# A selective-scan block on one core: the scan writes into PSUM, and its product is taken there

## The chip, the core and the metric

The kernel runs on one core of a Trainium2 chip. The core has a matrix engine (TensorE, PE in the profile), a vector engine (VectorE, DVE), an activation engine (ScalarE, ACT) and a general engine (GpSimd, POOL); DMAs are mostly issued from a fifth queue (SP). Each engine works through its own queue in order. The metric is the device time of one execution in microseconds (us).

## The reference

The input is 4096 rows of 1024 numbers. The block is a half feed-forward step, a Mamba step and the same feed-forward step again, each with a layer norm and a residual:

```python
x = x + 0.5 * ffn(layernorm(x))
x = x + mamba(layernorm(x))
x = x + 0.5 * ffn(layernorm(x))
```

The feed-forward step multiplies by a weight matrix rounded to -1, 0 or 1 times a scale, and adds a bias. The Mamba step is what the change touches:

```python
u, z = split(x @ W_in.T)                  # 1024 channels each
u = silu(conv_b + causal convolution of u over 4 rows)
dt_r, B, C = split(u @ W_xproj.T)         # 64, 16 and 16 columns
dt = softplus(dt_r @ W_dt.T + b_dt)
# for each of 16 states n and each channel d, along the rows t:
h[t] = exp(dt[t] * A[d, n]) * h[t-1] + dt[t] * B[t, n] * u[t]
y[t] = sum over n of h[t] * C[t, n]
out = ((y + u * Dskip) * silu(z)) @ W_out.T
```

So for each state there is a linear recurrence along the rows (the exponential is its decay), and a product of the whole history h with C.

## The kernel before

The rows are cut into 16 chunks of 256 rows (T). Channels lie on the 128 partitions, in 8 blocks; a chunk is worked in two halves of 4 blocks (HB). The history of a state is a tile `h` of 4 x 256 columns in SBUF. For each chunk, half and state:

- `fetch` loads the state's rows of B and C, spread over all partitions (`bc`, 6 buffers), through SP.
- `enter` (L934, L941) lets GpSimd write u * dt * B into `h` and add to each block's first column what comes over from the chunk before.
- `decaying` (L913) lets ScalarE write the decays, exp(dt * A), into a PSUM tile `da` of 2 blocks (512 columns, one of 3 such buffers). Two `da` tiles, j = 0 and 1, serve one state. Column 0 of each block is left out: it stays 0, set once before the loop (L847), so that a scan over two blocks starts anew at each of them.
- `recur` (L966) lets VectorE scan 512 columns: h = da * h_before + h, in place in `h`. After that the `da` buffer is free.
- `leave` (L949) lets ScalarE copy the last column of all 4 blocks of `h` into `state`, which the next chunk's `prepare` reads.
- `left` (L981) lets VectorE take the product of the whole `h` (1024 columns) with C into a tile `p`. It stands one state behind: the product of state n - 1 comes between the two scans of state n.
- `paired` (L996) adds, for states 0, 4 and 8, the product before to this one, on VectorE. It too stands one state behind, after the second scan.
- `summed` (L1019) lets TensorE transpose the remaining products and sum them in PSUM; `gate` (L1036) multiplies by silu(z) on VectorE.

All the rest runs beside it: the feed-forward steps (`ffn`: L456 and L458 split the normalized rows into two parts, L499 multiplies, L479 adds the result), the norm statistics (L393 to L412), the convolution (L550 and L560), the products with W_in (L616 and L675) and W_out (L758, added at L729), the delta step (L720), `prepare` (L860 to L873) and `skipping` (L899, u * Dskip as a further product).

The order of all instructions on each engine is fixed when the program is built. `Streams` is a small planner: each piece of work is a generator that asks for an engine for a planned time (`dve(1132)` asks VectorE for 1132 ns) and not before a given time. The planner always gives the engine to the request that can start first; among equals, to the one of lowest rank. The ranks (DECAY, ENTER, RECUR and so on), REACH (planned time from one engine to another), the LATE constants (added to due times), HOLD (how long an engine may be kept free for a request of lower rank) and the planned DMA times (5000 and 6000 ns) set that order; at run time only semaphores hold an engine. A second rule keeps instructions marked "port" on VectorE and GpSimd apart in the plan. There are 3 PSUM buffers `bank` for everything that TensorE writes apart from the sums.

Of the kernel before, what the change touches and what calls it, by code (L numbers as in the profile page):

```python
# [32 lines left out]
F32 = mybir.dt.float32  # L33
F32R = mybir.dt.float32r
AF = mybir.ActivationFunctionType
ALU = mybir.AluOpType
# [16 lines left out]
FULL, PASS, TURN = 0.844, 0.455, 0.855  # L53
REACH = 160
ISSUE, ADDED = 950, 6000
SWITCH = 1300

LATE_P, LATE_X, LATE_D, LATE_N = 300, 300, 1200, 300
PAIRED = (0, 4, 8)

DECAY, ENTER, SUM, PREPARE, RECUR, GATE = 4, 3, 1, 0, 5, 0
FFN_A, NORM, U_PART, CONV, DELTA, OUT, FFN_C = 1, 1, 3, 2, 2, 2, 3

HOLD = 250, 0, 0, 500
Z = 2, 4


class Streams:
# [32 lines left out]
    def run(self):  # L101
        hold = dict(zip(("PE", "DVE", "ACT", "POOL"), HOLD))
        while self.streams:
            todo = sorted(((self.start(s[2]), s[1], i) for i, s in enumerate(self.streams)))
            for at, rank, i in todo:
# [72 lines left out]
def macaron_mamba_kernel(  # L178
# [165 lines left out]
    def streamed(load, n, ahead, rank):  # L344

        queue = []

        def fill():
            for i in range(n):
                yield lambda: 0 if len(queue) < ahead else INF  # L350
                w = yield from weights.take()
                load(i, w)
                queue.append((order.now + 5000, w))

        order.spawn(fill(), rank)
        return queue
# [53 lines left out]
    def normed(c, ln, xn, t, at):  # L410
        end = yield act(D + 210, at)
        nc.scalar.activation(  # L412
            xn[t],
            x_tiles[c, t],
            AF.Identity,
            scale=ln[:, 28 + t : 29 + t],
            bias=ln[:, 32 + t : 33 + t],
        )
        return xn[t], end + REACH + LATE_N

# [21 lines left out]
    def ffn(c, which, rank, at, tiles=range(TT)):  # L442
# [3 lines left out]
        def split(t):  # L446
# [6 lines left out]
            def cut(g, pt, at_):  # L453
                part_hi, part_lo = (flat(p_[:, 4 * g : 4 * g + 4, :]) for p_ in (hi, lo))
                end = yield act(512, at_)
                nc.scalar.copy(part_hi, pt)  # L456
                end = yield dve(640, end + REACH)
                nc.vector.tensor_tensor(part_lo, pt, part_hi, ALU.subtract)  # L458
                banks.put(pt, end)
                ends.append(end)  # L460
                if len(ends) == NB // 4:
                    ready["parts", key, t] = end + REACH + LATE_N
                    parts[t] = lo, hi
# [195 lines left out]
    def gates(c, xT):  # L659
        queue = streamed(z_weights, NB, 2, Z[0])  # L660
        for half in range(2):
# [110 lines left out]
    def back():  # L772
        for c in range(NC - 1):
            yield OUT
            yT = []
            for half in range(2):
                if half:
                    yield from when("product", c, 1, 0)
                    queue = streamed(lambda i, w: out_weights(i // 2, i % 2, w), NB, 3, OUT)
                yT.append((yield from us.take()))  # L780
                yield from turned(c, half, yT[half])
# [62 lines left out]


    for _, da in decays.free:
        nc.vector.memset(da[:, :, 0], 0.0)  # L847
    halves = [(c, half) for c in range(NC) for half in range(2)]
# [54 lines left out]
    def decaying():  # L903
        for c, half, n in items:
# [3 lines left out]
            for j in range(2):  # L908
                da = yield from decays.take()
                for i in range(2):  # L910
                    b = 2 * j + i
# [13 lines left out]
    def enter():  # L925
        for c, half, n in items:
# [15 lines left out]
            entering[c, half, n] = h  # L942
            ready["enter", c, half, n] = end + REACH
            if n + 1 == NST:
                overs.put(over[c, half], end)

    def leave(c, half, n, h, at):
        end = yield act(100, at)
        nc.scalar.copy(state[:, half, :, n], h[:, :, T - 1])  # L949
        ready["left", c, half, n] = end  # L950
        if n + 1 == NST:
            ready["state", c, half] = end

    def recur():
        behind = None
        for c, half, n in items:
# [4 lines left out]
            for j in range(2):  # L961
# [3 lines left out]
                rows_ = flat(h[:, 2 * j : 2 * j + 2, :])  # L965
                nc.vector.tensor_tensor_scan(rows_, flat(da), rows_, 0.0, ALU.mult, ALU.add)  # L966
                decays.put(da, end)
                if behind and j == 0:
                    yield from left(*behind)
                elif behind:  # L970
                    yield from paired(*behind[:3])
            order.spawn(leave(c, half, n, h, end + REACH), ENTER)
            behind = c, half, n, h
        yield from left(*behind)
        yield from paired(*behind[:3])

    def left(c, half, n, h):
        bc = coming.pop((c, half, n))
        p = yield from products.take()
        end = yield dve(1132, 0, True)  # L980
        nc.vector.tensor_tensor(p, h, bc[:, 1:2, :].to_broadcast([P, HB, T]), ALU.mult)  # L981
# [138 lines left out]
```

## Time and profile before

| what | value |
|---|---|
| time, median of 2 runs | 2623.18 us (2622.4 and 2623.95) |
| time of the profiled execution | 2623.95 us |
| its span, first to last instruction | 2622.2 us |
| mean granted TensorE clock | 0.980 |
| decay exponentials on ScalarE, L913 | 2048, 474 ns each |
| scans on VectorE, L966 | 1024, 1206 ns each |
| products on VectorE, L981 | 512, 1355 ns each |
| pair sums on VectorE, L996 | 96, 2014 ns each |
| entering products on GpSimd, L934 | 512, 2391 ns each |
| state copies on ScalarE, L949 | 512, 188 ns each |

The profile comes from one execution. A group line names the line of the kernel, the engine, the operation, what it writes and reads, the shapes and the count; after the bar stand the busy time in us and the mean duration of one in ns, and after the second bar the idle time of the engine just before such instructions, with what ended it. The first scan starts at 102.1 us and the last at 2576.3 us; between them the 16 chunks follow each other with a period of about 156 us.

### The profile page before, as it was taken

To read this page: it belongs to the slowest core of one execution; us is meant where nothing else is said; L and a number is where in the kernel's file an instruction comes from. 1 tells how busy PE (TensorE), PEld (TensorE's weight loads), DVE (VectorE), ACT (ScalarE), POOL (GpSimd) and SP (SyncE) were. 2 spreads that over 40 slices of the span, in tenths; PEclk is the share of its full clock that TensorE was granted. 3 is DMA by queue.
4 is the path that set the end of the run, shared out by engine and by line. 5 is a ranking of instruction groups with operands and counts; after the bars stand their busy time and mean duration, and the time that the engine had idled before them with its cause. 6 is when DMAs were issued, how large, how long until landed. Compare 5 with 4: busy or idle time off the path is not lost. (4 is left out here: it accounts for less than half of the span.)

```text
span 2622.2 us, 38817 instructions
## 1 busy us (share of the span) xinstructions
PE 2473.1 (94%) x13314; PEld 2118.7 (81%) x13314; DVE 2467.7 (94%) x2532; ACT 1953.2 (74%) x4084; POOL 1746.9 (67%) x1433
## 2 busy tenths in 40 slices
PE   5987999999999999999999999999999999999867
PEld 4776778888888888888888888888888888888756
DVE  5589999999999999999999999999999999999994
ACT  3678678787778878777797878779787887876652
POOL 0456767767676776767677676766767677776772
PEclk9999899999999999999999999999999999999988
DMA  5544445556544555555555544555654455554451
GB/s 166 156 134 129 149 128 174 158 176 181 165 150 141 177 165 176 160 169 151 156 164 181 173 152 153 160 166 163 188 165 146 141 175 159 177 175 151 122 156 37
DMA packets 218541, 410.68 MB, mean 157 GB/s; under 512 B 19172, under 2 KB 85860, under 8 KB 218344
## 3 DMA queue, kind: packets, MB, share of 16 engines
q1 hardware_dynamic: 209128, 374.65, 44.2%
q0 software_dynamic: 9216, 33.56, 6.9%
q8 instruction: 105, 1.72, 0.3%
q14 instruction: 92, 0.75, 0.1%
HBM read 390.82 MB, written 17.31 MB: 156 GB/s over the span
## 5 line engine op out<-in xcount | busy, mean ns | idle before, releaser
L934 POOL TENSOR_TENSOR h<-u,bc 128x1024 f32<-128x1024 f32 x512 | 1224.2, 2391 | 565.8 <-ACT da L913 257.7
L913 ACT ACTIVATE da<-dt,pr 128x255 f32<-128x255 f32 x2048 | 946.3, 474 | 432.1 <-DVE h L966 398.9
L966 DVE TENSOR_TENSOR_SCAN h<-da,h 128x512 f32<-128x512 f32 x1024 | 1215.5, 1206 | 31.8 <-ACT da L913 22.3
L981 DVE TENSOR_TENSOR p<-h,bc 128x1024 f32<-128x1024 f32 x512 | 694.0, 1355 | 0.1
L1019 PE MATMUL y<-ident,p 128*128 128x128 f32 x3584 | 480.7, 279 | 74.2 <-DVE p L981 59.9
L1019 PEld LDWEIGHTS y<-ident,p 128*128 128x128 f32 x3584 | 423.0, 144 | 136.8 <-DVE p L981 81.1
L616 PE MATMUL bank<-xT,weight 128*128 128x259 f32 x2048 | 477.4, 386 | 11.1 <-issue 7.6
L675 PE MATMUL bank<-weight,xT 128*128 128x256 f32 x2048 | 478.0, 382 | 2.9 <-DMA weight<-in_w_in 1.0
L758 PE MATMUL bank<-weight,u 128*128 128x256 f32 x2016 | 464.1, 380 | 2.9 <-DMA weight<-in_w_out 2.8
L616 PEld LDWEIGHTS bank<-xT,weight 128*128 128x128 f32 x2048 | 384.0, 192 | 73.5 <-issue 10.8
L675 PEld LDWEIGHTS bank<-weight,xT 128*128 128x128 f32 x2048 | 377.5, 191 | 51.8 <-DVE x L479 2.9
L758 PEld LDWEIGHTS bank<-weight,u 128*128 128x128 f32 x2016 | 373.9, 191 | 49.5 <-ACT da L913 2.5
L941 POOL TENSOR_TENSOR h<-h,over 128x4 f32<-128x4 f32 x512 | 343.0, 670 | 33.7
L499 PE MATMUL bank<-wf,lo 128*128 128x512 f32 x976 | 255.7, 404 | 3.8 <-DVE lo L458 3.7
L499 PE MATMUL bank<-wf,hi 128*128 128x512 f32 x976 | 244.7, 393 | 0.0
L499 PEld LDWEIGHTS bank<-wf,lo 128*128 128x128 f32 x976 | 181.1, 190 | 44.3 <-DVE lo L458 8.0
L560 DVE SCALAR_TENSOR_TENSOR u<-bank,pr,u 128x256 f32<-128x256 f32 x384 | 176.4, 467 | 38.7 <-ACT u L550 36.4
L499 PEld LDWEIGHTS bank<-wf,hi 128*128 128x128 f32 x976 | 181.5, 188 | 37.2 <-issue 0.3
L996 DVE TENSOR_TENSOR p<-p,p 128x1024 f32<-128x1024 f32 x96 | 193.4, 2014 | 0.0
L395 POOL TENSOR_SCALAR ln<-ln 128x1 f32<-128x1 f32 x96 | 35.8, 373 | 182.0 <-ACT tmp L393 178.7
L428 PE MATMUL bank<-ident,tmp 128*128 128x128 f32 x756 | 114.5, 285 | 33.1 <-ACT tmp L412 24.0
L428 PEld LDWEIGHTS bank<-ident,tmp 128*128 128x128 f32 x756 | 93.1, 146 | 52.8 <-ACT tmp L412 30.2
(98 smaller groups left out, 1966.5 us busy)
## 6 DMA issues: line engine op xcount, KB each, us to landing
bc<-bcd SPq DMA_DIRECT2D x512, 256.0 KB, 3.7
weight<-in_w_in SPq DMA_DIRECT2D x128, 512.0 KB, 4.6
weight<-in_w_in SPq DMA_DIRECT2D x256, 256.0 KB, 5.6
weight<-in_w_out SPq DMA_DIRECT2D x128, 512.0 KB, 4.1
x<-hbias POOLq DMA_DIRECT2D x64, 512.0 KB, 9.4
x<-in_x SPq DMA_DIRECT2D x32, 512.0 KB, 5.0
out<-x SPq DMA_DIRECT2D x30, 512.0 KB, 4.5
weight<-in_w_ffn SPq DMA_DIRECT2D x5, 512.0 KB, 7.2
```

The lines of the kernel that those rows point to most:

```text
L428: nc.tensor.matmul(pt[:, j * P : (j + 1) * P], xn[:, k * P : (k + 1) * P], ident, start=(j == 0), stop=(j == 3), is_transpose=True, skip_g ...
L499: nc.tensor.matmul(pf, x[:, k, :], wf[:, k, cols], start=(x is lo and k == 0), stop=(x is hi and k == NB - 1),)
L616: nc.tensor.matmul(pp[:, : KER - 1 + T], wt[:, k, :], xT[:, k, PAD - KER + 1 : PAD + T], start=(k == 0), stop=(k == NB - 1),)
L675: nc.tensor.matmul(pp[:, t, :], xT[:, k, PAD + t * P : PAD + (t + 1) * P], wt[:, :, i, :], start=(k == 0 and t == 0), stop=(k == NB - 1), ...
L758: nc.tensor.matmul(po[:, t, :], yT[:, b, t * P : (t + 1) * P], wt[:, b, :], start=(half == 0 and t == 0 and b == 0), stop=(half == 1 and b ...
L913: nc.scalar.activation(da[:, i, 1:], dt[c, half][:, b, 1:], AF.Exp, scale=a_neg[:, half * HB + b, n : n + 1],)
L934: nc.gpsimd.tensor_tensor(h, u[c, half], bc[:, 0:1, :].to_broadcast([P, HB, T]), ALU.mult)
L941: nc.gpsimd.tensor_tensor(h[:, :, 0], h[:, :, 0], over[c, half][:, :, n], ALU.add)
L966: nc.vector.tensor_tensor_scan(rows_, flat(da), rows_, 0.0, ALU.mult, ALU.add)
L981: nc.vector.tensor_tensor(p, h, bc[:, 1:2, :].to_broadcast([P, HB, T]), ALU.mult)
L996: nc.vector.tensor_tensor(flat(p), flat(p), flat(q), ALU.add)
L1019: nc.tensor.matmul(y[t][:, b * P : (b + 1) * P], p[:, b, t * P : (t + 1) * P], ident, start=(first and b == 0), stop=(n == NST - 1 and b = ...
```

## The change

The scan now writes its result over the decays in the PSUM tile `da` and no longer into `h`. The product with C reads it there, 512 columns at a time, directly behind each scan on VectorE; so there are 1024 products of 512 columns in place of 512 of 1024, and the pair sum follows the second product of its own state. `h` is free after the second scan. The state copy is made per `da` tile, 2 blocks at a time, by ScalarE (1024 copies in place of 512), and `da` is free after both the copy and the product. Since the scan overwrites column 0 of each block, ScalarE zeroes the two columns anew in each `da` tile before the exponentials, by a copy from a tile of zeros (1024 copies of 128 x 2). With it come other planning constants: REACH 300 in place of 160, ranks, LATE constants, later planned DMA times, a term TABLE that puts ScalarE requests for another function table 300 ns later in the planner's choice, three z weights ahead in place of two, and the output weights fetched from product 12 of the second half on in place of product 0. The diff, without the lines that only rename or move:

```diff
-REACH = 160
-ISSUE, ADDED = 950, 6000
+REACH = 300
+ISSUE, ADDED = 950, 9000
-LATE_P, LATE_X, LATE_D, LATE_N = 300, 300, 1200, 300
+LATE_P, LATE_X, LATE_D, LATE_E = 300, 700, 1200, 300
-DECAY, ENTER, SUM, PREPARE, RECUR, GATE = 4, 3, 1, 0, 5, 0
-FFN_A, NORM, U_PART, CONV, DELTA, OUT, FFN_C = 1, 1, 3, 2, 2, 2, 3
-
-HOLD = 250, 0, 0, 500
+DECAY, ENTER, SUM, PREPARE, RECUR, GATE = 1, 1, 1, 0, 5, 1
+FFN_A, NORM, U_PART, CONV, DELTA, OUT, FFN_C = 1, 0, 3, 2, 2, 2, 4
+
+TABLE = 300
+HOLD = 250, 0, 100, 500
...
-            todo = sorted(((self.start(s[2]), s[1], i) for i, s in enumerate(self.streams)))
+            todo = []
+            for i, s in enumerate(self.streams):
+                w = s[2]
+                other = not callable(w) and w[0] == "ACT" and w[3] not in (None, self.table)
+                todo.append((self.start(w) + other * TABLE, s[1], i))
+            todo.sort()
...
-                queue.append((order.now + 5000, w))
+                queue.append((order.now + 6500, w))
...
-        return xn[t], end + REACH + LATE_N
+        return xn[t], end + REACH
...
-                    ready["parts", key, t] = end + REACH + LATE_N
+                    ready["parts", key, t] = end + REACH
...
-        queue = streamed(z_weights, NB, 2, Z[0])
+        queue = streamed(z_weights, NB, 3, Z[0])
...
-                    yield from when("product", c, 1, 0)
+                    yield from when("product", c, 1, 12)
...
-    for _, da in decays.free:
-        nc.vector.memset(da[:, :, 0], 0.0)
+    none = const.tile([P, 2], F32, name="none")
+    nc.vector.memset(none, 0.0)
...
                 da = yield from decays.take()
+
+                yield act(0)
+                nc.scalar.copy(da[:, :, 0], none)
...
-            ready["enter", c, half, n] = end + REACH
+            ready["enter", c, half, n] = end + REACH + LATE_E
...
-    def leave(c, half, n, h, at):
-        end = yield act(100, at)
-        nc.scalar.copy(state[:, half, :, n], h[:, :, T - 1])
-        ready["left", c, half, n] = end
-        if n + 1 == NST:
+    def leave(c, half, n, j, da, at):
+
+        blocks = slice(2 * j, 2 * j + 2)
+        end = yield act(0, at)
+        nc.scalar.copy(state[:, half, blocks, n], da[:, :, T - 1])
+        if j and n + 1 == NST:
             ready["state", c, half] = end
+        decays.put(da, max(end, (yield from when("multiplied", c, half, n, j))))
...
                 da = decay.pop((c, half, n, j))
                 end = yield dve(1132)
                 rows_ = flat(h[:, 2 * j : 2 * j + 2, :])
-                nc.vector.tensor_tensor_scan(rows_, flat(da), rows_, 0.0, ALU.mult, ALU.add)
-                decays.put(da, end)
-                if behind and j == 0:
-                    yield from left(*behind)
-                elif behind:
-                    yield from paired(*behind[:3])
-            order.spawn(leave(c, half, n, h, end + REACH), ENTER)
-            behind = c, half, n, h
-        yield from left(*behind)
-        yield from paired(*behind[:3])
-
-    def left(c, half, n, h):
-        bc = coming.pop((c, half, n))
-        p = yield from products.take()
-        end = yield dve(1132, 0, True)
-        nc.vector.tensor_tensor(p, h, bc[:, 1:2, :].to_broadcast([P, HB, T]), ALU.mult)
-        bcs.put(bc, end)
-        product[c, half, n] = p
-        if n not in PAIRED:
-            ready["product", c, half, n] = end + REACH + LATE_P
-        order.spawn(give(c, half, n, h, end), ENTER)
+                nc.vector.tensor_tensor_scan(flat(da), flat(da), rows_, 0.0, ALU.mult, ALU.add)
+                order.spawn(leave(c, half, n, j, da, end + REACH), 0)
+                yield from left(c, half, n, j, da)
+            hs.put(h, end)
+
+    def left(c, half, n, j, da):
+        bc = coming[c, half, n]
+        if not j:
+            product[c, half, n] = yield from products.take()
+        p = product[c, half, n][:, 2 * j : 2 * j + 2, :]
+        end = yield dve(605)
+        nc.vector.tensor_tensor(p, da, bc[:, 1:2, :].to_broadcast([P, 2, T]), ALU.mult)
+        ready["multiplied", c, half, n, j] = end
+        if j:
+            bcs.put(coming.pop((c, half, n)), end)
+            if n not in PAIRED:
+                ready["product", c, half, n] = end + REACH + LATE_P
+            yield from paired(c, half, n)
...
-    def give(c, half, n, h, at):
-        end = yield from when("left", c, half, n)
-        hs.put(h, max(at, end))
```

More of the change, by code (lines that the diff above doesn't have):

```diff
@@ L942, in enter @@
             entering[c, half, n] = h
-            ready["enter", c, half, n] = end + REACH
+            ready["enter", c, half, n] = end + REACH + LATE_E
             if n + 1 == NST:
                 overs.put(over[c, half], end)
-    def leave(c, half, n, h, at):
-        end = yield act(100, at)
-        nc.scalar.copy(state[:, half, :, n], h[:, :, T - 1])
-        ready["left", c, half, n] = end
-        if n + 1 == NST:
+    def leave(c, half, n, j, da, at):
[3 more added lines that the diff above has]
+        if j and n + 1 == NST:
             ready["state", c, half] = end
+        decays.put(da, max(end, (yield from when("multiplied", c, half, n, j))))
     def recur():
-        behind = None
         for c, half, n in items:
```

## The prediction

> **What bounds the kernel now.** I read the page first: which engine is full, and over the whole span or only in part of it.
>
> ```profile
> span 2622.2 us, 38817 instructions
> PE 2473.1 (94%) x13314; PEld 2118.7 (81%) x13314; DVE 2467.7 (94%) x2532; ACT 1953.2 (74%) x4084; POOL 1746.9 (67%) x1433
> ```
>
> Two engines stand at 94%. The windows view, cut to the length of one chunk (156 us; the columns are busy time and instruction count of PE, PEld, DVE, ACT, POOL), shows the steady state without start and end:
>
> ```profile
> 1044.00:1200.00 156.00, 152.94 (x839) 131.43 (x838) 153.59 (x158) 122.58 (x259) 109.29 (x90) 1.00 0.55 164
> 1200.00:1356.00 156.00, 152.95 (x838) 131.40 (x838) 153.65 (x158) 122.64 (x258) 109.29 (x90) 1.00 0.54 163
> 1356.00:1512.00 156.00, 152.94 (x838) 131.46 (x837) 153.70 (x157) 122.65 (x257) 109.39 (x90) 1.00 0.53 163
> ```
>
> So VectorE works 153.6 and TensorE 152.9 of 156 us, at full clock. VectorE's busy time can't fall by more than about 3 us per chunk before TensorE takes over, while anything added to VectorE is paid in full. ScalarE has 33 us free. Where VectorE's time goes, and what ScalarE's free time is, come from the groups of VectorE and the waits of ScalarE in the window 1200 to 1356:
>
> ```profile
> L966 DVE TENSOR_TENSOR_SCAN h<-da,h 128x512 f32<-128x512 f32 x65 | 77.2, 1206 | 1.0 <-ACT da L913 0.7 <-POOL h L941 0.2
> L981 DVE TENSOR_TENSOR p<-h,bc 128x1024 f32<-128x1024 f32 x33 | 44.7, 1354 | 0.0
> L996 DVE TENSOR_TENSOR p<-p,p 128x1024 f32<-128x1024 f32 x6 | 12.2, 2037 | 0.0
> L560 DVE SCALAR_TENSOR_TENSOR u<-bank,pr,u 128x256 f32<-128x256 f32 x24 | 10.9, 466 | 0.1
> L458 DVE TENSOR_TENSOR lo<-bank,hi 128x512 fp32r<-128x512 f32 x8 | 5.3, 676 | 0.2 <-ACT hi L456 0.2
> ```
> ```profile
> ACT da L913 <- DVE h L966: 22.5, 19, 2.5
> ```
>
> Scans and products are four fifths of VectorE. ScalarE waits 22.5 us per chunk for a decay buffer: it runs ahead, and VectorE waits for it 0.7 us.
>
> A record is longer than what it costs, because records of neighbours overlap. The timeline of VectorE gives the cost, start to start:
>
> ```profile
> 57.48 1.52 DVE L560 SCALAR_TENSOR_TENSOR u<-bank,pr,u 128x256 f32<-128x256 f32 x3 [16.22 <-ACT u L550]
> ...
> 1288.48 0.47 DVE L560 SCALAR_TENSOR_TENSOR u<-bank,pr,u 128x256 f32<-128x256 f32 x1
> 1288.88 0.67 DVE L458 TENSOR_TENSOR lo<-bank,hi 128x512 fp32r<-128x512 f32 x1
> 1289.48 0.47 DVE L560 SCALAR_TENSOR_TENSOR u<-bank,pr,u 128x256 f32<-128x256 f32 x1
> ```
> ```profile
> 2572.92 2.32 DVE L966 TENSOR_TENSOR_SCAN h<-da,h 128x512 f32<-128x512 f32 x2
> 2575.17 1.19 DVE L981 TENSOR_TENSOR p<-h,bc 128x1024 f32<-128x1024 f32 x1
> 2576.28 1.21 DVE L966 TENSOR_TENSOR_SCAN h<-da,h 128x512 f32<-128x512 f32 x1
> 2577.58 1.23 DVE L981 TENSOR_TENSOR p<-h,bc 128x1024 f32<-128x1024 f32 x1
> ```
>
> What to see: L560 alone advances the engine by 1288.88 - 1288.48 = 0.40 us. At 57.48 three of them each read what the one before wrote: (1.52 - 0.47) / 2 = 0.525 each, so a result taken by the next instruction costs 0.13. A scan advances it by (2575.17 - 2572.92) / 2 = 1.13; the very last product needs the scan just in front of it and comes 2577.58 - 2576.28 = 1.30 after it: 0.17 more. An undisturbed product of 1024 columns takes 2576.28 - 2575.17 = 1.11 to 1.12, a 512-column instruction with one input in PSUM 1289.48 - 1288.88 = 0.60.
>
> **The change part by part**, per chunk (64 scans, 32 states), against the profiled execution's 2623.95 us (span 2622.2 and 1.75 around it; the median of the runs is 0.8 below).
>
> *Product removed:* 32 times the mean record less the usual overlap, 1.354 - 0.075 = 1.28: 40.9 us. Of it 32 x (1.28 - 1.12) = 5.1 is time in which GpSimd holds the product up: the timeline has a pair sum of 2.88 us from 1323.90 on, while GpSimd's L934 ran until 1325.70, 1.08 before its end.
>
> *Product added:* 64 of 512 columns, one input in PSUM: the nearest row is L458, 0.60, so 38.4. Alone this saves 2.5. It should not be held up as L981 was (1189 to 2781 ns): L458, with one input in PSUM and one in SBUF as here, has no long record in the trace (657 to 693 ns).
>
> *The new dependence:* before, a product ran one state behind, so a scan of the next state stood between it and its input. Now each product reads what the scan just in front wrote. The rows price it at 0.13 (L560) and 0.17 (the last product); between L319 and L321, 0.78 start to start against 0.67 for a record of 0.75 less its overlap, it is 0.11. I take 0.15. It costs nothing where another instruction stands between. The recurrence has the lowest rank, so any of the other 54 VectorE instructions of a chunk (24 + 8 + 8 + 8 + 4 + 2) that is ready goes first; the scan is 1.13 of a slot's 1.73, so up to 35 of them fall there, at least none. They come in bunches: I take 24 slots covered, 40 x 0.15 = 6.0; ends 29 x 0.11 = 3.2 and 64 x 0.17 = 10.9. Behind the waiting product stand all of VectorE's other instructions, and TensorE's transposes wait for it.
>
> The Trainium skill says of this (VectorE: DVE Perf Modes, The DRAIN you can't avoid) that a semaphore between VectorE instructions "costs nothing extra". By that the 6.0 would be 0 and the sum 2597; the rows above say 0.11 to 0.17, and the sum goes by them.
>
> *The pair sums* (L996, 6 per chunk) now follow directly on the product they read: 6 x 0.13 = 0.8. Their hold-ups, 6 x (1.96 - 1.12) = 5.0, may stay, as GpSimd's work is the same; from -5.0 to 0, I take 0.
>
> *Scan into PSUM:* no row has VectorE writing a large tile there. ScalarE's 255 columns into PSUM take 474 ns against 494 for 256 into SBUF (L899); VectorE's 512 columns from PSUM 0.60 against half of 1.12. So -0.02 to +0.04 per scan, -1.3 to +2.6; I take 0, the ends lying on both sides.
>
> *ScalarE:* 64 zeroings of 128x2, and 64 state copies in place of 32. A state copy advances ScalarE by 0.10 (copy at 1379.51, next exponential at 1379.61) with a record of 0.19. 96 x 0.10 = 9.6, at most 19. It is covered by the 22.5 of waiting for buffers; without that cover 9.6 would be paid, since ScalarE would have 132 of 156.
>
> *Buffer return:* a decay buffer now comes back after scan, product and copy instead of after the scan, about 0.75 + 0.1 us later. But product and scan alternate now, so two filled buffers are still two scans and two products of work (3.7 us with the waits, against 3.5 to 4.8 before). A switch of tables for the softplus takes 1.28 + 1.57 + 1.28 = 4.1 us, so a wait of some tenths can come at 6 such places: 0 to 4.5 (6 x 0.75); I take 0, as before only 0.7 was lost.
>
> *Order:* state tiles come free at the second scan, earlier, which helps only GpSimd (109 of 156). SP's fetches move with the plan: a third z weight ahead, the output weights from product 12 instead of 0, still three states (15 us, at 156 / 32 each) ahead of their use, when they land in 4 to 6 us. The new reach, late and rank constants cost nothing themselves but re-order all queues; not priced, -2 to +2.
>
> Sum per chunk: -40.9 + 38.4 + 6.0 + 0.8 = +4.3, VectorE being the bound. Times 16: +69, so 2623.95 + 69 = 2693.
>
> **The rivals.**
>
> *A, faster: freed from GpSimd.* The dependence is hidden or cheap, and the pair sums lose their hold-ups too: -2.5 - 5.0 = -7.5, of which TensorE's 152.9 lets through about 2.7: 16 x 2.7 = 43, 2581. For it: the long records of L981 and L996. Against: three rows that price the dependence. It decides where the mean wait per slot falls below (2.5 - 0.8) / 64 = 0.03 us.
>
> *B, ScalarE becomes the bound.* The plan puts the copy 0.3 us after the scan, where the product on the same bank runs to 0.75 after it. If the copy has to wait for the product, ScalarE loses up to 0.45 in order, 64 times: 28.8, so 122.6 + 9.6 + 28.8 = 161.0, against 151.9 that VectorE's steps sum to now: +9.1, or 2770. The exponentials, the copies out of banks and the activations all queue behind it. For it: stretches in which ScalarE is already busy 18 to 19 of 19.5 us. Against: a late ScalarE finds the product done and doesn't wait, and this wait partly replaces the 22.5 it already has.
>
> The Trainium skill (PSUM — Partial Sum Buffer, PSUM bank collisions raise a hardware error) says that two engines must be kept from using one bank and quadrant at once, "reads against reads included"; no run here shows it, and by it B's wait is certain to exist, though not that it decides.
>
> *C, no change that counts.* The dependence is mostly covered (3.2), relief at the pair sums and re-ordering pay for the rest: -2.5 + 3.2 + 0.8 - 1.5 = 0: 2624.
>
> That the change doesn't do what it says is no rival: in the code the product's input is the decay tile that the scan has just written.
>
> **How the numbers follow.** Forecast 0.50 (its own range 2648 to 2771, by the ends of the dependence wait: -2.5 + 0.8 + 3.2 = +1.5 and -2.5 + 0.8 + 10.9 = +9.2 per chunk), A 0.15, B 0.17, C 0.18. The predicted time is 2693. For 8 in 10 the range reaches into A and B: 2585 to 2780. This kernel's measurement can tell about 2%, that is 2571 and 2676. Faster: 0.10, from A with TensorE's gaps shrinking as well. Same: the rest of A, C and a fifth of the forecast, 0.33. Slower: 0.57.
>
> **What would show it.** L560's neighbours aside, a scan followed by its product start to start: 1.28 to 1.30 if I am right, 1.13 if A is. The new product's records at 0.66 to 0.70 us with no long ones. VectorE busy 156 to 158 per chunk of about 160, or idle in front of the product. ScalarE's waits: if they now stand at the state copy and VectorE's waits for the decays grow beyond some us per chunk, B. TensorE busy 153 of a shorter period: A. I am wrong if a scan into PSUM takes other than 1.13, or if the new order covers nearly every scan with other work.

## The result, and the profile after

The changed kernel takes 2837.78 us (median of 2 runs, 2837.64 and 2837.93) against 2623.18: a ratio of 1.0823, with a 95% interval of 1.0791 to 1.0854. It is slower, as forecast, by 215 us instead of 69, and outside the range that ended at 2780. All that follows is set against the spans, 2836.0 us after and 2622.2 before; they differ by 213.8.

The page of the kernel after, span and busy time of each engine:

```profile
span 2836.0 us, 40701 instructions
PE 2534.8 (89%) x13314; PEld 2130.2 (75%) x13314; DVE 2514.0 (89%) x3042; ACT 2163.1 (76%) x5592; POOL 1549.0 (55%) x1433
```

No engine stands at 94% any more. VectorE has 2514.0 - 2467.7 = 46.3 us more to do, but 2836.0 - 2514.0 = 322.0 us of idle time in place of 154.5. The windows view, cut to about the new length of a chunk (170 us, columns as before), shows the same in the steady state:

```profile
1580.00:1750.00 170.00, 156.27 (x839) 131.21 (x838) 155.93 (x191) 135.41 (x352) 96.56 (x89) 1.00 0.49 149
```

VectorE and TensorE are both idle for 14 us of such a stretch, where before each was idle for 2 to 3 of 156. Taken from the first scan of a chunk to that of the next, a chunk lasts 168.8 us (1120.6 to 1289.4) against 155.0 before (1199.8 to 1354.8). VectorE is busy for 154.7 us of it against 152.7 before: 2 us more, a little under the forecast (156 to 158 against 153.6, so 2.4 to 4.4 more). The other 12 us per chunk are idle time. TensorE's granted clock does not make them: its mean is 0.974 against 0.980, and in this window it is 1.00, as it was before. The groups of VectorE and the waits of ScalarE, in the window 1580 to 1750 of the kernel after:

```profile
L975 DVE TENSOR_TENSOR_SCAN da<-da,h 128x512 f32<-128x512 f32 x65 | 79.4, 1222 | 4.3 <-ACT da L917 3.8 <-POOL h L949 0.4
L986 DVE TENSOR_TENSOR p<-da,bc 128x512 f32<-128x512 f32 x65 | 44.7, 688 | 2.0
L1002 DVE TENSOR_TENSOR p<-p,p 128x1024 f32<-128x1024 f32 x6 | 11.9, 1976 | 0.1
L566 DVE SCALAR_TENSOR_TENSOR u<-bank,pr,u 128x256 f32<-128x256 f32 x25 | 11.7, 469 | 2.0 <-ACT u L556 1.9
L464 DVE TENSOR_TENSOR lo<-bank,hi 128x512 fp32r<-128x512 f32 x8 | 5.2, 686 | 3.4 <-ACT hi L462 3.4
```
```profile
ACT state L959 <- DVE p L986: 21.1, 24, 3.3
ACT da L917 <- DVE p L986: 6.1, 7, 1.1
```

Read the last column of the groups against that of before: the scan waits 4.3 us where it waited 1.0, the convolution (L566, before L560) 2.0 where it waited 0.1, the split of the rows (L464, before L458) 3.4 where it waited 0.2. All three wait for ScalarE. Summed over the whole trace, VectorE's waits that ScalarE ends are 197.4 us, against 83.5 before; those that TensorE ends are 65.4 against 43.7. ScalarE's own wait for a decay buffer has become a wait of the state copy for the product on the same buffer: 21.1 us, and 6.1 at the zeroing.

The timeline of VectorE, near the end of the kernel after (start, record):

```profile
2768.79 1.22 DVE L975 TENSOR_TENSOR_SCAN da<-da,h 128x512 f32<-128x512 f32 x1
2770.04 0.69 DVE L986 TENSOR_TENSOR p<-da,bc 128x512 f32<-128x512 f32 x1
2770.65 1.22 DVE L975 TENSOR_TENSOR_SCAN da<-da,h 128x512 f32<-128x512 f32 x1
2771.78 0.73 DVE L485 SCALAR_TENSOR_TENSOR x<-bank,hscl,x 128x512 f32<-128x512 f32 x1
2772.42 0.68 DVE L986 TENSOR_TENSOR p<-da,bc 128x512 f32<-128x512 f32 x1
```

Scan to its own product, start to start: 2770.04 - 2768.79 = 1.25. Scan to another instruction: 2771.78 - 2770.65 = 1.13. Product to the next scan: 0.61. Over the whole trace the direct step occurs 707 times with a median of 1.26, so the wait costs 0.13 x 707 = 92 us. About 0.09 of each 0.13 is the overlap of records that no longer takes place and is counted as busy; 0.04 is idle, 28 us. The steps that the prediction priced thus come to 46.3 + 28 = 74 us. What is left, 213.8 - 74 = 140 us, is idle time of VectorE in other places: 322.0 - 154.5 - 28 = 139.5. By the sums above, 197.4 - 83.5 = 114 of it are waits for ScalarE.

Where such time lies, in one stretch of the trace after, ScalarE first and VectorE below it:

```profile
1438.30 1.28 ACT L572 ACT_TABLE_LOAD   x1
1439.59 1.06 ACT L572 ACTIVATE u<-u 128x1024 f32<-128x1024 f32 x1
1440.56 1.69 ACT L904 ACTIVATE p<-u,pr 128x256 f32<-128x256 f32 x4
...
1444.91 1.06 ACT L700 ACTIVATE sz<-sz 128x1024 f32<-128x1024 f32 x1
1445.87 1.54 ACT L462 CAST hi<-bank 128x512 fp32r<-128x512 f32 x3
1447.43 1.28 ACT L921 ACT_TABLE_LOAD   x1
1448.73 0.99 ACT L921 ACTIVATE da<-dt,pr 128x255 f32<-128x255 f32 x2
```
```profile
1442.36 0.69 DVE L986 TENSOR_TENSOR p<-da,bc 128x512 f32<-128x512 f32 x1
1443.76 0.69 DVE L464 TENSOR_TENSOR lo<-bank,hi 128x512 fp32r<-128x512 f32 x1 [0.71 <-ACT hi L462]
1446.47 1.89 DVE L464 TENSOR_TENSOR lo<-bank,hi 128x512 fp32r<-128x512 f32 x3 [2.02 <-ACT hi L462]
1449.81 1.23 DVE L975 TENSOR_TENSOR_SCAN da<-da,h 128x512 f32<-128x512 f32 x1 [1.46 <-ACT da L917]
```

ScalarE works without a break through its other activations between two loads of its function table, and writes no decay from 1438.3 to 1448.7. The three decay buffers are scanned out by 1442.4; after that VectorE waits 0.71 + 2.02 + 1.46 us, for the split rows and then for a decay.

### The profile page after: what moved, and what is told of

It is laid out like the page before. It is cut to its first block, busy times and chain, and to the rows that moved or that the text cites. A ratio compares the mean times of both kernels' runs of the same rounds, so it can differ in the third digit from the quotient of the medians.

```text
span 2836.0 us, 40701 instructions
## 1 busy us (share of the span) xinstructions
PE 2534.8 (89%) x13314; PEld 2130.2 (75%) x13314; DVE 2514.0 (89%) x3042; ACT 2163.1 (76%) x5592; POOL 1549.0 (55%) x1433
## 5 line engine op out<-in xcount | busy, mean ns | idle before, releaser
L942 POOL TENSOR_TENSOR h<-u,bc 128x1024 f32<-128x1024 f32 x512 | 1228.1, 2399 | 701.6 <-DVE da L975 660.2
L975 DVE TENSOR_TENSOR_SCAN da<-da,h 128x512 f32<-128x512 f32 x1024 | 1250.9, 1222 | 68.1 <-ACT da L917 44.6
L921 ACT ACTIVATE da<-dt,pr 128x255 f32<-128x255 f32 x2048 | 977.4, 477 | 60.5
L986 DVE TENSOR_TENSOR p<-da,bc 128x512 f32<-128x512 f32 x1024 | 704.7, 688 | 42.2 <-ACT state L959 7.4
L1021 PE MATMUL y<-ident,p 128*128 128x128 f32 x3584 | 486.4, 279 | 64.5 <-DVE p L1002 45.1
L959 ACT COPY state<-da 128x2 f32<-128x2 f32 x1024 | 159.8, 157 | 379.3 <-DVE p L986 347.1
L681 PEld LDWEIGHTS bank<-weight,xT 128*128 128x128 f32 x2048 | 386.0, 194 | 77.0 <-DVE x L485 21.5
L505 PE MATMUL bank<-wf,lo 128*128 128x512 f32 x976 | 259.4, 409 | 41.7 <-DVE x L485 17.7
L505 PEld LDWEIGHTS bank<-wf,lo 128*128 128x128 f32 x976 | 182.0, 193 | 96.5 <-DVE x L485 28.0
L917 ACT COPY da<-none 128x2 f32<-128x2 f32 x1024 | 165.6, 162 | 111.6 <-DVE p L986 97.0
L505 PE MATMUL bank<-wf,hi 128*128 128x512 f32 x976 | 244.9, 393 | 0.0
L566 DVE SCALAR_TENSOR_TENSOR u<-bank,pr,u 128x256 f32<-128x256 f32 x384 | 180.0, 470 | 59.8 <-ACT u L556 57.1
L505 PEld LDWEIGHTS bank<-wf,hi 128*128 128x128 f32 x976 | 181.4, 188 | 45.5 <-issue 8.0
L434 PE MATMUL bank<-ident,tmp 128*128 128x128 f32 x756 | 125.3, 302 | 93.3 <-ACT tmp L418 26.0
L1002 DVE TENSOR_TENSOR p<-p,p 128x1024 f32<-128x1024 f32 x96 | 198.2, 2065 | 2.4
```

The costliest lines, as they stand in the source:

```text
L434: nc.tensor.matmul(pt[:, j * P : (j + 1) * P], xn[:, k * P : (k + 1) * P], ident, start=(j == 0), stop=(j == 3), is_transpose=True, skip_g ...
L505: nc.tensor.matmul(pf, x[:, k, :], wf[:, k, cols], start=(x is lo and k == 0), stop=(x is hi and k == NB - 1),)
L566: nc.vector.scalar_tensor_tensor(ub, pp[:, k : k + T], tap, ub, ALU.mult, ALU.add)
L681: nc.tensor.matmul(pp[:, t, :], xT[:, k, PAD + t * P : PAD + (t + 1) * P], wt[:, :, i, :], start=(k == 0 and t == 0), stop=(k == NB - 1), ...
L921: nc.scalar.activation(da[:, i, 1:], dt[c, half][:, b, 1:], AF.Exp, scale=a_neg[:, half * HB + b, n : n + 1],)
L942: nc.gpsimd.tensor_tensor(h, u[c, half], bc[:, 0:1, :].to_broadcast([P, HB, T]), ALU.mult)
```

## The experiments

The theories at the start: T1, rival B's, that ScalarE is held at the state copy by the product on the same buffer, so that the loss belongs to the change itself; T2, that the new planning constants make the loss; T3, that the work of the copies on ScalarE does. Later ones are named where they arise. Each run was timed beside the kernel before; the ratios are to that, with 95% intervals.

**The constants and the structure apart.** e1 is the kernel after with all planning constants of before; e2 is the kernel before with those of after:

```diff
# e1 (e2 is the reverse, on the kernel before)
-REACH = 300
-ISSUE, ADDED = 950, 9000
+REACH = 160
+ISSUE, ADDED = 950, 6000
...
-DECAY, ENTER, SUM, PREPARE, RECUR, GATE = 1, 1, 1, 0, 5, 1
+DECAY, ENTER, SUM, PREPARE, RECUR, GATE = 4, 3, 1, 0, 5, 0
...
-TABLE = 300
+TABLE = 0
```

> The changed kernel with all planning constants (reach, late terms, ranks, holds, the table term, planned DMA times, prefetch points) set back to those of before. Theory 1, the new waits between VectorE and ScalarE (a product that follows its scan, copies and zeroings that ScalarE holds back until the product is done) are the cost: 2780 to 2900 us, VectorE idle still 10 us or more of a chunk. Theory 2, the new constants make a worse order: 2700 or less, near the forecast of 2693.

> The kernel before with the new planning constants and nothing else of the change. Theory 1: 2600 to 2670 us. Theory 2: over 2720, at least half of the 214 us that were lost.

e1: 3024.97 us, 1.1535 (1.1517 to 1.1552). e2: 2737.83 us, 1.0442 (1.0427 to 1.0458). e1 is the end of T2 in its plain form (the constants of before make things worse) and lies above T1's window as well; e2 has T2's number and not T1's. Both are slower than the kernel whose constants they left: the new constants are worth -187 us on the new structure and +115 on the old one, so each set belongs to its structure, and no theory had that. The order by itself moves this kernel by more than all priced steps together. In e1, and later in e4, TensorE's granted clock is lower as well (0.930 and 0.942, against 0.974); what that adds to their times was not separated.

**The copies.** e3 leaves out the state copies and the zeroings and is planned anew; e4 plans the state copy behind the product instead of behind the scan; e5 keeps the order of the kernel after, instruction by instruction, and only doesn't issue the copies and zeroings:

```diff
# e3 and e5
-                nc.scalar.copy(da[:, :, 0], none)
...
-        nc.scalar.copy(state[:, half, blocks, n], da[:, :, T - 1])
# e3 and e4
-        end = yield act(0, at)
+        end = yield from when("multiplied", c, half, n, j)
# e4 too
+        end = yield act(0, end + REACH)
```

> The changed kernel without the state copies and without the zeroings: the state stays 0 and the scans of a pair of blocks run on with what stands in column 0, so this part of the computation is left out; a decay tile is free after its product. Theory 1, and theory 3 (the mere number of ScalarE's instructions): 2680 to 2720 us, what is left being the wait of the product for its scan, VectorE idle under 5 us per chunk. Theory 2: 2800 or more.

> The changed kernel with each state copy planned after the product on the same bank and no longer 300 ns after the scan, so that ScalarE's fixed order doesn't reach it early. Theory 1: ScalarE's wait of 22 us per chunk at the state copies falls to under 8, and the time to 2700 to 2780 us. Theory 3 (the buffers and the number of instructions, not the place of the copy): 2810 to 2860.

> The changed kernel in exactly its planned order, but with state copies and zeroings not issued (the state stays 0 and column 0 keeps what stands there; this part of the computation is left out). Theory 5, ScalarE being held behind the product for copies, zeroings and the return of the bank makes the 12 us of VectorE idle per chunk: 2740 us or less. Theory 4, the plan does not know of the wait of each product for its scan, and the engines run an order that was laid out for shorter steps: 2790 to 2840.

e3: 2808.09 us, 1.0710 (1.0694 to 1.0726). e4: 2948.87 us, 1.1245 (1.1226 to 1.1263). e5: 2792.81 us, 1.0659 (1.0643 to 1.0675). e3 lies 88 us above the window of T1 and T3, and where T2 had it (2800 or more); e4 lies 169 above T1's window and 89 above T3's. e5 was to part T5 (ScalarE held behind the product by copies, zeroings and the later return of the buffer, 2740 at most) from T4 (the order is wrong since the plan doesn't know the wait of the product for its scan, 2790 to 2840): without a single copy, and with everything else in place, 45 of the 215 us go and 170 stay. T4 has the number. T5 falls as far as copies and zeroings go; the later return of the buffer is still there in e5, as the waits of ScalarE show. First e4, then e5:

```profile
ACT state L960 <- DVE p L987: 386.8, 436, 4.2
```
```profile
ACT da L922 <- DVE p L986: 642.2, 567, 4.4
```

Planned later, the copy waits for the product as long as ever (347.1 us in the kernel after). Left out, its wait moves on to the exponential that needs the same buffer, which waits 642.2 us: ScalarE is still held behind the product. It has 263 us less to do in e5 (1899.7 against 2163.1), and its wait takes up most of that time; the length of a wait alone is no price. Nor are the 45 us all that the copies did. VectorE's waits for ScalarE fall by 64 us in e5, from 197.4 to 133.3, but its pair sums take 32 us more than in the kernel after (198.2 there):

```profile
L1002 DVE TENSOR_TENSOR p<-p,p 128x1024 f32<-128x1024 f32 x96 | 230.5, 2401 | 2.4
```

T1 in its form with the copies alone, and T3, fall as the whole cause.

**The product away from PSUM.** e6 keeps the order of the kernel after, but its product reads `h` in SBUF, and so not what the scan has just written. e7 keeps the order too; its scan stays in `h`, and product and copy read it there:

```diff
# e6 and e7
-        nc.vector.tensor_tensor(p, da, bc[:, 1:2, :].to_broadcast([P, 2, T]), ALU.mult)
+        nc.vector.tensor_tensor(p, rows_, bc[:, 1:2, :].to_broadcast([P, 2, T]), ALU.mult)
# e7 too
-                nc.vector.tensor_tensor_scan(flat(da), flat(da), rows_, 0.0, ALU.mult, ALU.add)
+                nc.vector.tensor_tensor_scan(rows_, flat(da), rows_, 0.0, ALU.mult, ALU.add)
-        nc.scalar.copy(state[:, half, blocks, n], da[:, :, T - 1])
+        nc.scalar.copy(state[:, half, blocks, n], rows_[:, :, T - 1])
```

> The changed kernel in exactly its planned order, but the product takes its input from the tile h in SBUF, which the scan only reads (so the product is of the input of the recurrence and not of its result; this part of the computation is left out). The product then waits for no scan and doesn't touch the bank. Theory 4: 2740 us or less, since 707 waits of 0.13 us go, even if GpSimd holds some products up. Theory 5: also lower, 2700 to 2780. A third way, that neither matters: 2800 to 2850.

> The changed kernel in exactly its planned order, with the scan written back to h as before, and product and state copy taken from there, still directly behind the scan: the wait of the product for its scan stays, the bank is free after the scan. Theory 5: 2700 to 2760 us. Theory 4: 2800 to 2900, the products now being held up by GpSimd as well.

e6: 3042.97 us, 1.1607 (1.1588 to 1.1627). e7: 3288.79 us, 1.2547 (1.2529 to 1.2566). Both lie above every window. In both, the products have both inputs in SBUF and take some 446 us more in all (1151.4 and 1149.0 against 704.7). In both, too, the plan hands `h` to GpSimd's next refill at the time of the scan, as in the kernel after, so what is read from it later can be that of the refill (in e7 the last column copied too), and the copy of e7 waits 625.3 us for GpSimd. As tests of the wait, and of a buffer that is free after the scan, they tell nothing, for these changes outweigh it. The product's group, in e6 and then in e7:

```profile
L986 DVE TENSOR_TENSOR p<-h,bc 128x512 f32<-128x512 f32 x1024 | 1151.4, 1124 | 0.0
```
```profile
L986 DVE TENSOR_TENSOR p<-h,bc 128x512 f32<-128x512 f32 x1024 | 1149.0, 1122 | 34.0
```

The same 512 columns in the same place take 1124 and 1122 ns with both inputs in SBUF, and 688 ns with one of them in PSUM. That GpSimd makes the difference shows in the single records: in e6 the 559 products that do not overlap GpSimd's L942 in time take 668 ns (median, at most 683), the 465 that do take 1749; in the kernel after, the 716 that overlap it and the 308 that do not both take 691. So the change does free the product from GpSimd, as the prediction had it; only there is little gained by it, since in the order of before the product was held up by just 0.16 us each.

**How much a bare re-ordering does.** e8 alters one constant of the kernel after by 10 ns:

```diff
-REACH = 300
+REACH = 310
```

> The changed kernel with the planned time from engine to engine 310 ns in place of 300: no instruction differs, only the order. If the time hangs mainly on which order comes out of the planner: 30 us or more away from 2838, in either direction. If the waits of the change set it whatever the order: 2820 to 2855.

e8: 2903.74 us, 1.1081 (1.1064 to 1.1097), 66 us above the kernel after with the same instructions, where the expectation by order had it (30 us or more away). The lost time has moved: VectorE's wait for the feed-forward results (L485 after TensorE's L505) is now 105.5 us, against 32.0.

**Is it that the plan doesn't know the wait?** (T4.) The planner counts 1132 + 605 ns for a scan and its product, and they take 1.26 + 0.60 us. e9 tells it the wait; e10 tells it also the zeroings and the exponentials' true steps, with constants searched anew for the shortest planned end; e11 is the kernel after with constants found by the same search, and nothing told; e12 the kernel before with such constants:

```diff
# e9
-                yield from left(c, half, n, j, da)
+                yield from left(c, half, n, j, da, end + 130)
# e10 too
-                yield act(0)
+                yield act(150)
...
-                    end = yield act(T + 150, 0, "exp")
+                    end = yield act(T + 165, 0, "exp")
```

> The changed kernel with one thing told to the planner: the product is due 130 ns after its scan and not at once (other work may go between). The planner lays its last instruction at 2714 us of its own time, against 2654 for the changed kernel and 2628 for the kernel before, which took 184 us more than that and 5 us less. Theory 4, the run is longer than its plan because the plan doesn't know of the wait: 2740 to 2800 us, that is 30 to 90 above the plan, and shorter than the changed kernel although its plan is longer. If the untold wait is not the cause, the gap stays at 160 to 200: 2875 to 2915.

> The changed kernel with the planner told of the product's wait (130 ns), of the zeroing (225 ns in place of 100) and of the exponentials (451 in place of 438 ns), and with planning constants chosen anew so that its plan is short (2593 us of planned time). Theory 4: 2640 to 2710 us, most of the loss gone. If the gap stays whatever the plan is told: 2760 to 2790.

> The changed kernel, told nothing, with planning constants chosen anew by the same kind of search for a short plan (2565 us of planned time). Theory 4: the gap stays at 150 to 220, so 2715 to 2785 us, longer than the told one although its plan is 28 us shorter. If a short plan is all that counts: 2600 to 2640.

> The kernel before with planning constants chosen anew by the same kind of search (2553 us of planned time). It shows what an equal search gives without the change. Theory 4: the order before has no product behind its own scan, so the gap is small, 0 to 60: 2553 to 2615 us. TensorE's 153 us per chunk are a floor near 2570.

e9: 2880.14 us, 1.0990 (1.0973 to 1.1006). e10: 2744.17 us, 1.0471 (1.0455 to 1.0486). e11: 2802.84 us, 1.0695 (1.0677 to 1.0713). e12: 2654.23 us, 1.0124 (1.0108 to 1.0139). The wait alone told makes it 42 us slower (e9), the new search alone 35 faster (e11); all told and searched anew gives the best kernel with the change that was found, 94 us under the change as made and still 121 over the kernel before. How the 94 divide between telling and search is not shown, for e10 and e11 have different constants. e9 lies where it should if the untold wait is not the cause (2875 to 2915). e10 lies above T4's window (2640 to 2710) and under the other (2760 to 2790); e11 and e12 miss theirs upwards, both being further from their planned end than any theory had it. T4 is a part of the cause at most. The page of e10 and its groups show where those 121 are:

```profile
PE 2510.2 (92%) x13314; PEld 2130.9 (78%) x13314; DVE 2555.9 (93%) x3042; ACT 2147.1 (78%) x5591; POOL 1550.7 (57%) x1433
```
```profile
L975 DVE TENSOR_TENSOR_SCAN da<-da,h 128x512 f32<-128x512 f32 x1024 | 1249.8, 1221 | 11.2 <-ACT da L921 7.7 <-POOL h L949 2.0 <-ACT da L917 0.5
L986 DVE TENSOR_TENSOR p<-da,bc 128x512 f32<-128x512 f32 x1024 | 704.5, 688 | 68.7 <-ACT state L959 29.5 <-DVE da L975 0.5 <-issue 0.4
L1002 DVE TENSOR_TENSOR p<-p,p 128x1024 f32<-128x1024 f32 x96 | 255.3, 2660 | 2.8
```

VectorE is busy 88.2 us more than before, 61.9 of which are the pair sums: 2660 ns each in place of 2014. Its idle time is 186.8 us, 32.3 more than before, and the scans wait less than before (11.2 against 31.8). So with this plan most of the extra idle time is gone, and the price that stays is the dependence, paid partly at the product, and the pair sums. These read two tiles of SBUF and are held up by GpSimd: in the kernel after, the 24 that do not overlap L942 take 1224 ns (median) and the 72 that do 2656; in e10 all 96 overlap it (2762).

**Is this order unlucky, or any order of the new structure?** (O: any order is worth tens of microseconds by chance, in both structures; F: only the new structure loses by a disturbed order.) Each structure got the same two treatments: a step of 10 ns in REACH (e13 before, 170 for 160; e14 after, 290 for 300), and an order from searched constants of nearly equal planned end (e15 before, e16 after):

```diff
# e13
-REACH = 160
+REACH = 170
# e14
-REACH = 300
+REACH = 290
```

> The kernel before with REACH at 170 instead of 160 ns; every instruction of VectorE costs what it cost, only the planned order differs (planned end 2632 us, against 2628 for the kernel before). Theory O (any planned order is worth tens of microseconds by chance, in the old structure as in the new): 2640 to 2720 us. Theory F (the old structure bears a disturbed order, and only the new one loses by it, since a chain of decay, scan and product through one PSUM buffer has less slack): within 15 us of the kernel before, 2608 to 2640 us.

> The changed kernel with REACH at 290 instead of 300 ns (planned end 2714 us); the order alone differs. Theory O: anywhere from 2760 to 2930 us, as 310 gave 2904. Theory F: the same, 2760 to 2930; its part of the test is the run of the old structure beside it. Both fall if it lands below 2740 us, where the priced steps alone would put it: then the order of 300 ns is a bad one by itself.

> The kernel before in a second order from re-searched constants (planned end 2574 us), with a table load put into the plan. Theory O: between 2640 and 2700 us, since the order of planned end 2553 gave 2654. Theory F: 2610 to 2650 us.

> The changed kernel in a second order from re-searched constants (planned end 2575 us), the wait behind each scan not in the plan. Theory O with the priced steps (+69): its time lies 70 to 110 us over the old structure's run of nearly the same planned end beside it. Theory F: 140 us or more over it.

e13: 2626.51 us, 1.0019 (1.0009 to 1.0028). e14: 2907.75 us, 1.1087 (1.1066 to 1.1108). e15: 2619.31 us, 0.9990 (0.9980 to 0.9999). e16: 2836.49 us, 1.0817 (1.0799 to 1.0835). The pairs differ by 281 and 217 us. All four lie where F has them, and of those that could part the two (e13, e15, e16) none lies where O has it. The order of the kernel after is not a bad pick among its like, and the clock is no rival either: e16 has a granted clock of 0.984, more than before (0.980), and loses as much as the kernel after. F needs a bound, though: e2 and e12 show that the old structure loses as well, 115 and 34 us against the runs beside them, under other constants. The windows view, 1400 to 2000 us, of e15 and then of e16:

```profile
1400.00:2000.00 600.00, 586.12 (x3202) 502.72 (x3201) 592.00 (x606) 479.71 (x985) 452.40 (x343) 1.00 0.54 162
```
```profile
1400.00:2000.00 600.00, 546.70 (x2921) 455.95 (x2920) 546.72 (x660) 470.50 (x1222) 333.94 (x308) 1.00 0.49 150
```

TensorE and VectorE are filled to 586 and 592 of 600 us in the one, and idle 53 us each in the other; they wait on each other and on ScalarE (over the whole of e16, TensorE 114 us for VectorE's products and pair sums, VectorE 99 us for TensorE's L505 and 98 for ScalarE). Where VectorE loses it is a matter of the order. For the results of L505 e16 loses more than twice as much as the kernel after, and at the scans much less:

```profile
L975 DVE TENSOR_TENSOR_SCAN da<-da,h 128x512 f32<-128x512 f32 x1024 | 1250.2, 1221 | 14.2 <-ACT da L917 6.3 <-ACT da L921 6.0 <-POOL h L949 1.3
L485 DVE SCALAR_TENSOR_TENSOR x<-bank,hscl,x 128x512 f32<-128x512 f32 x124 | 91.7, 740 | 101.0 <-PE bank L505 99.0 <-PE bank L536 1.8
```

**Does any unplanned work on VectorE cost a multiple of itself?** (G: yes; S: no, the multiple comes with the shared buffer.) e17 is the kernel before in its exact order, with a small zero fill behind each scan that the plan doesn't know; e18 has the same fills in the plan:

```diff
# e17 and e18, behind the scan
+                nc.vector.memset(junk[(2 * n + j) % 4], 0.0)
# e18 too
-                end = yield dve(1132)
+                end = yield dve(1215)
```

> The kernel before in its exact order, with one instruction more behind each of the 1024 scans: VectorE sets 128x48 of an unused SBUF tile to zero, by an estimate from the rows of the 128x2 and 128x128 settings of the first microseconds (steps 0.05 and 0.14 us) some 0.08 us each, 85 us in all, which nothing waits for and the plan does not know. That is about what the change lengthens VectorE by (46 us of work and 42 us of idle time in front of the products). Theory G (VectorE and TensorE are both filled to 98% in this order, so work that the plan does not know costs a multiple of itself, whatever it is): 2790 to 2860 us. Theory S (a filler costs itself, and the multiple comes from the chain of decay, scan, product and copies through one PSUM buffer): 2700 to 2730 us.

> The same filler behind each scan, its 83 ns in the plan (planned end 2700 us against 2628). Theory G: 2690 to 2740 us, near the plan again, at least 50 us under the run in which the plan does not know it. Theory S: 2690 to 2740 us too, but within 25 us of that run.

e17: 2630.26 us, 1.0030 (1.0018 to 1.0042). e18: 2700.19 us, 1.0301 (1.0281 to 1.0322). The filler missed its planned size. Its group in e17:

```profile
L969 DVE MEMSET junk<- 128x48 f32 x1024 | 100.4, 98 | 0.0
```

Scan to fill to next instruction takes 1.17 + 0.02 = 1.19 us where scan to next took 1.13, so the fills put in about 0.06 x 1024 = 61 us and not 85. VectorE's busy time rose only from 2467.7 to 2486.2, by 18.5, mainly because the products were shorter (1315 ns on the mean against 1355, 20.5 us in all); the span rose by 7.1. That is against a multiple at this size: the old order absorbs most of what is put in. It says nothing of 85 us, and both windows were missed downwards; G and S are not told apart at the size that counts. e18 lies in the window that both share, but neither had it above e17. It shows the order's weight once more: the instructions are those of e17, the plan counts 85 us for the fills where e17 shows 61, and the kernel is 70 us slower.

## Why the prediction was wrong

- **Product removed and added: right.** Records of 688 ns (forecast 660 to 700), the longest 694, a step of 0.60 to 0.61 as taken. No long records.
- **The dependence: right.** Forecast 40 x 0.15 = 6.0 us per chunk; measured 44 x 0.13 = 5.7. The Trainium skill (VectorE: DVE Perf Modes, The DRAIN you can't avoid) says of its own test, eight `tensor_copy` with a semaphore after each, that the semaphore "costs nothing extra here"; here, 707 steps of 1.26 against 1.13 show a cost, and the three rows of the trace before had it right.
- **Scan into PSUM: right.** The step is 1.13, into PSUM as into SBUF; the mean record grew by 16 ns (1222 against 1206), inside the range given.
- **Pair sums: right in this kernel** (193.4 to 198.2 us), not in others of the same structure (255.3 in e10).
- **ScalarE's copies, "covered by the 22.5 of waiting for buffers": wrong.** Without them the kernel is 45 us faster (e5), 2.8 per chunk, and VectorE's waits for ScalarE are 64 us shorter. One part was mis-sized as well: a zeroing and the step to the exponential behind it take 0.20 us, not 0.10.
- **Rival B** had ScalarE's time right: 135.4 us busy and 21.1 + 6.1 waiting for the product make 162.6 of the 170 in the window, against the 161.0 worked out. Its signs came too: ScalarE waits at the state copy, and the scan waits 4.3 us in place of 1.0. But its price (2770) is too small, and that the copy's wait decides is refuted by e5: with no copy to wait, 170 of the 215 us remain. That ScalarE is held behind the product by the buffer alone is not refuted.
- **"Anything added to VectorE is paid in full"** held in neither structure: e17 paid 7.1 us of span for 18.5 of busy time, the change 214 for 74.
- **The failed step** is the last line of the sum, "VectorE being the bound", with the terms that were put at nothing to get there: the copies as covered, the buffer's return ("I take 0") and the order ("not priced, -2 to +2"). The priced steps gave +74 us (forecast 69). The runs showed 140 us more in idle time of VectorE, 8.7 per chunk, 114 of them in waits for ScalarE. Leaving out the copies in the same order takes off 45 (e5); the other 95 belong to the order and the buffer's return together, and no run separates these two. The new constants are not to blame by themselves: with the old ones the change costs 187 us more (e1). VectorE's steps bound the kernel only as long as it is fed 98% of the time, and that was so in three orders of the old structure (before, e13 and e15) and in none of the new. In every full kernel of the new structure tried (nine orders, 2744 to 3025 us) VectorE was idle for 187 to 464 us; in the old structure, filler runs aside (five orders, 2619 to 2738), for 138 to 282.

That the time came out slower, as forecast, is in part luck: the priced 69 us are there, but they are a third of the loss.

What is shown: the loss beyond the priced steps is VectorE idle time (139.5 us in the trace), most of it in waits for ScalarE; the copies are 45 of the 215; it is no accident of the one order (e13 to e16) and not the clock; telling the planner the true steps and searching anew brings 94 back, and then the pair sums take 62. What is not shown is which property of the new structure lets every plan slip. A buffer that stays taken by product and copy for about 0.75 us longer, and queues in which scan and product alternate, fit the traces, but this was only argued: e7, in which the buffer was free after the scan, let other waits in, and a fourth decay buffer wasn't tried.

## What to carry to other kernels

Here two engines were both filled to 98%, and all nine orders of the new structure ended above the sum of its instruction costs (2693 us). In such a kernel price the order too, by running both structures under a slightly disturbed plan (here 10 ns in one constant was worth 5 us in the old structure, and 66 and 70 in the new). Leaving out what waits tells more than the length of its wait: the copies at which ScalarE waited 347 us were worth 45, and the wait moved on to the next instruction on the same buffer. When a change makes a plan's hidden assumptions false (a step that depends on the one just before, a buffer held longer), measure those steps, tell them to the planner and search its constants anew before judging the change; telling it one of them alone (e9) made things worse.

## What the runs showed of the hardware

- A VectorE instruction that reads what the one just in front wrote starts 0.13 us later than another would (1.26 against 1.13, 707 times); about 0.09 of it is the overlap of neighbouring records that falls away.
- A product of 512 columns of fp32 takes 688 ns, at most 694, with one input in PSUM, and 1124 ns on the mean with both in SBUF, in the same order beside the same instructions of GpSimd (e6): 668 where it does not overlap GpSimd's product and 1749 where it does (medians).
- A zero fill of 48 columns behind a scan has records of 98 ns and delays the next instruction by 0.06 us; 1024 of them lengthened the span by 7.1 us (e17).
